# Projections of queries and keys in four column tiles of 32 instead of one product on the whole array, in both attentions of a two-layer macaron block

## The chip, the cores and the metric

The kernel runs on one core of a Trainium2 chip. The metric is the device time of one execution in microseconds: the median of 3 runs. A profile of one further execution shows what each engine did. TensorE is the matrix engine (PE in the profile; its weight loads are PEld), VectorE is DVE, ScalarE is ACT, GpSimd is POOL, SyncE is SP. All arithmetic is in f32.

## The reference

The input x is 2 x 2048 x 256. Six layers are added to it one after the other, each on a layer norm of x:

```python
x = x + 0.5 * L0_ffn(layernorm(x))    # mixture of 6 experts (top 2) plus a shared one
x = x + L0_attn(layernorm(x))         # full attention, 16 heads of 16
x = x + 0.5 * L0_ffn(layernorm(x))
x = x + 0.5 * L1_ffn(layernorm(x))    # gated recurrence of 2 steps, then tanh
x = x + L1_attn(layernorm(x))         # causal, rotary, relative positions within 32
x = x + 0.5 * L1_ffn(layernorm(x))
```

The change concerns the first products of the two attentions, for each of the 2 sequences:

```python
q = x @ Wq.T * (1.0 / sqrt(256))      # L0; in L1 the scale is 1/4, behind the rotation
k = x @ Wk.T
scores = einsum('bqhd,bkhd->bhqk', q, k)
attn = softmax(scores)
out = einsum('bhqk,bkhd->bqhd', attn, v)
```

In the second attention q and k are rotated in pairs of neighbouring features before the scores.

## The kernel before

x stays in on-chip memory for the whole run, in 32 chunks of 128 tokens; a block is 4 chunks (512 tokens). The normed input of a block is turned so that features lie on partitions: `xnT`, two tiles of 128 features x 512 tokens.

**One projection.** Heads are handled in groups of 4 (`G` = 4 groups). The weights are laid out so that one product of 128 output columns holds two groups: on each strip of 32 partitions lie the 16 features of one head of one group and the 16 of a head of the other. `mm2` (L143 to L149) makes such a product: two matmuls, one for each 128 input features, into one PSUM bank of 128 x 512, on the whole 128 x 128 array. The profile's records have two MATMULs and two LDWEIGHTS for each f32 matmul, so a call of `mm2` is 4 of each. ScalarE then makes two tiles from the bank, one for each group, with a scale of 0 for the other group's rows (`part_rows`, L137). In the second attention `rotate` (L1009) copies the bank first, VectorE shuffles neighbouring rows, and the rotation is done by VectorE or GpSimd; `keys_out` and `queries_out` split the groups later.

**What surrounds it.** Every instruction goes out in the order of the program text; each engine works through its own list. The work of an attention is cut into half steps. In one half step of the first attention (loop at the end of `attention0`), TensorE gets, in this order:

- for each of 4 heads, a score product for the exponentials (`exponential`, L770: keys as weights, 512 queries stream) and one for the row maxima (`largest`, L756: queries as weights, 512 keys stream). These use 32 rows and 128 columns of the array, heads side by side on different rows;
- the jobs that are due in this step, from a list by step number (`jobs.at`): projections of later queries and keys, values (L604), transposes (L635, L658, L672, L125), output products (L681);
- the values weighted with the exponentials of an earlier half step (`weighted`, L782): 4 heads, each 128 rows and 32 columns of the array, side by side on different columns, into 32 partitions each of one bank.

In the second attention the order within a half step is: transposes of the band with the relative positions (L1218, L1222), score products (L1201, L1208, L1123), weighted values (L1237), and then the due jobs.

VectorE takes the maxima from PSUM (L760, L1131), ScalarE the exponentials (L775, L1229) and the copies of the weighted values (L644). All PSUM banks come from one pool of 8 (`bank()`), in order of use.

**The calls.** There are 64 calls in the two attentions: in each, 16 of queries (one for two groups of heads of a block) and 16 of keys. The callers are `keys` (L727) and `queries` (L746) of `attention0`, and `rotate` (L1013) of `attention1`. `mm2` itself stays for the shared expert and the recurrences. The router's product (`route`, L203) has a form of its own: for each half of the features, four products of 32 columns, into 32 partitions each of one bank; its four products stream four different tiles.

Of the kernel before, what the change touches and what calls it, by code (L numbers as in the profile page):

```python
# [17 lines left out]
P = 128  # L18
# [24 lines left out]
def macaron_kernel(ctx: ExitStack, tc: tile.TileContext, t: dict, out: bass.AP):  # L43
    nc = tc.nc
# [28 lines left out]
    def bank():  # L73
        return psum.tile([P, TB], F32, name="s")
# [59 lines left out]
    def rows(j):  # L134
        return slice(32 * j, 32 * j + 32)

    def part_rows(dst, src, i, bias):  # L137

        nc.scalar.activation(
            dst, src, AF.Identity, scale=rowsel[:, i : i + 1], bias=0.0 if bias is None else bias  # L140
        )

    def mm2(ps, w, cols, rhs, start=True, stop=True):  # L143

        for kc in range(2):
            nc.tensor.matmul(  # L146
                ps, lhsT=w[:, kc, cols], rhs=rhs[:, kc, :],
                start=start and kc == 0, stop=stop and kc == 1,
            )  # L149

# [14 lines left out]
    def moe(w, ws, gate_w, gate_b, rev, tri, iota, z, behind, last, gathered):  # L167
# [3 lines left out]
        with ExitStack() as s:  # L171
# [147 lines left out]
            def shared_part(b, i):  # L319
                ps = bank()  # L320
                mm2(ps, ws[:, :, i // 2 * D : i // 2 * D + D], ts(i % 2, P), xnT[b])
                if i < 2:
                    sgs = wk.tile([P, TB], F32, name="sgs", bufs=6)
                    nc.scalar.activation(sgs, ps, AF.Silu)
                    ps = sgs
                half.setdefault(b, []).append(ps)
# [380 lines left out]
    def attention0(norm, tail, rest, wq, wk_, wv, wo, bff):  # L707
# [7 lines left out]
        with ExitStack() as s:  # L715
            z = Pieces(s, "a0", norm, wo, bff)
# [7 lines left out]
            def keys(b, g, qc):  # L724

                pk = bank()
                mm2(pk, wk_, ts(g // 2, P), z.xnT(b, qc))  # L727
                for i in range(2):
                    if qc == 0:
                        kT[b, g + i] = kpool.tile([P, S], F32, name="kT", bufs=5)  # L730
                    part_rows(kT[b, g + i][:, ts(qc, TB)], pk, i, rowsel[:, 2 + i : 3 + i])
# [10 lines left out]
            def queries(t):  # L742

                b, qc, g = groups[t]
                pq = bank()
                mm2(pq, wq, ts(g // 2, P), z.xnT(b, qc))  # L746
                for i in range(2):
                    q[t + i] = wk.tile([P, TB], F32, name="q", bufs=4)
                    part_rows(q[t + i], pq, 4 + i, None)
                    mx[t + i] = wk.tile([P, CPB * J, SB], F32, name="mx", bufs=4)  # L750
# [42 lines left out]
            for b in range(B):  # L793
                first = b * SB * G * PER

                for qc in range(SB) if b else ():
                    for c in range(CPB):
                        at(first - 43 + 4 * qc + c, z.ln_stats, b, qc, c)
                    at(first - 37 + 4 * qc, z.ln_transpose, b, qc)
                for qc in range(0 if b else SB):  # L800
                    norm.xn.pop(qc)
                    at(-1, z.add_bias, qc)
                for g in range(0, G, 2):
                    for qc in range(SB):
                        at(first - 7 + PER * g + qc if b else (qc if g else -1), keys, b, g, qc)
                for half in range(2):
                    for qc in range(SB):
                        due = first + 1 + 16 * half + qc if b else 4 * half + qc
                        at(due, vals, b, half, qc)
            for t, (b, qc, g) in enumerate(groups):  # L810
                if t % 2 == 0:
                    at(PER * t - 2, queries, t)
                at(PER * t + 18, z.divide, t, b, qc, g, True)
                if g == G - 1:
                    at(PER * t + 19, z.outputs_T, b, qc)
                    at(PER * t + 20, z.outputs, b, qc, 0)
                    at(PER * t + 20, z.outputs, b, qc, 1)
# [161 lines left out]
    def attention1(norm, tail, w, relk, relv, kbias, dramp, skew):  # L979
# [4 lines left out]
        with ExitStack() as s:  # L984
            z = Pieces(s, "a1", norm, w["o"], None)
# [23 lines left out]
            def rotate(xa, wa, b, qc, g):  # L1009


                pa = bank()
                mm2(pa, wa, ts(g // 2, P), z.xnT(b, qc))  # L1013
                nc.scalar.copy(xa, pa)
                xb = wk.tile([P, TB], F32, name="s2", bufs=4)
                nc.vector.stream_shuffle(xb, xa, [i ^ 1 for i in range(32)])

                if step < 0:
                    nc.vector.tensor_tensor(xa, xa, cos[b, qc], ALU.mult)
                    nc.vector.tensor_tensor(xb, xb, sin[b, qc], ALU.mult)  # L1020
                    nc.vector.tensor_tensor(xa, xa, xb, ALU.add)
                else:
                    op = nc.gpsimd.tensor_tensor
                    z.later(1, op, xa, xa, cos[b, qc], ALU.mult)
                    z.later(2, op, xb, xb, sin[b, qc], ALU.mult)
                    z.later(3, op, xa, xa, xb, ALU.add)
# [3 lines left out]
            def keys(b, qc, g, own):  # L1030

                if qc == 0:
                    pair = features_slot()
                    kT[b, qc, g], kT[b, qc, g + 1] = pair[:, 0, :], pair[:, 1, :]
                    packed[b, qc, g] = kT[b, qc, g + 1]
                elif own:
                    packed[b, qc, g] = wk.tile([P, TB], F32, name="s2", bufs=4)
                else:
                    packed[b, qc, g] = keys_tile(b, qc, g + 1)
                rotate(packed[b, qc, g], w["k"], b, qc, g)  # L1040
# [22 lines left out]
            def queries(t):  # L1063

                b, qc, g = groups[t]
                for i in range(2):
                    q[t + 1 - i] = wk.tile([P, TB], F32, name="q", bufs=6)
                    mx[t + i] = wk.tile([P, CPB, J, MX], F32, name="mx", bufs=2)
                rotate(q[t + 1], w["q"], b, qc, g)
# [201 lines left out]
            for n, (b, qc, g) in enumerate(groups):  # L1271
                size = 2 * (qc + 1)
                start = Me[-1] + 1 if n else 0
                free = Es[n - NBAND] + (4 if groups[n - NBAND][1] else 2) if n >= NBAND else -9
                start = max(start, free + 5 - size)
                if n > 5 and n % 2 == 0:
                    start = max(start, Ee[n - 5] + 5)
# [3 lines left out]
                start = Me[-1] + 2  # L1281
                if n:
                    start = max(start, Ee[-1] + 1)
# [318 lines left out]
```

## Time and profile before

| | us |
|---|---|
| median of 3 runs | 4071.13 |
| lowest, highest | 4068.05, 4072.09 |
| the profiled execution | 4068.88 |
| its span on the core | 4067.0 |
| first attention, about | 340 to 2000 |
| second attention, about | 2570 to 3760 |

The granted clock of TensorE was 0.993 of full speed over the span. The costliest groups of matmuls in the page (line, engine, operation, names, rows*columns of the array, shape, count | busy us, mean ns of one | idle time before):

```profile
L756 PE MATMUL s<-kT,q 32*128 32x512 f32 x4096 | 1018.6, 618 | 1.9 <-DVE mx L760 1.9
L770 PE MATMUL s<-q,kT 32*128 32x512 f32 x4096 | 1013.0, 615 | 0.4 <-DVE q L639 0.4
...
L782 PE MATMUL s<-pT,v 128*32 128x512 f32 x4096 | 549.8, 605 | 0.6 <-ACT pT L775 0.2
```

In the names, the streamed tile stands ahead of the weights. A matmul that streams 512 columns is in flight for about 600 ns, but the next one of the same form starts before it is over; busy time counts the union. Four that lie side by side on different rows or columns of the array run at the same time, so a busy time is less than count times mean.

Times "at" a place are microseconds from the start of the span.

### The profile page before, as it was taken

The page shows a single profiled execution, that of the slowest core. Times are in us where ns is not written, and L with a number is a line of the kernel's source. Part 1 is how long each engine was busy: PE and PEld are TensorE (multiplying, and loading weights), DVE is VectorE, ACT ScalarE, POOL GpSimd, SP SyncE. Part 2 cuts the span into 40 slices and gives each one's busy share as a digit, 9 for nine tenths or more (in the row PEclk, how much of TensorE's full clock was granted, in tenths as well). Part 3 has the DMA queues.
Part 4 walks back from the last instruction along what each step waited for, and adds up shares of the span by engine and source line. Part 5 has one row for each costly group of instructions (what it writes and reads, how often), then busy time and mean ns, then how long its engine had stood idle before and what let it go on. Part 6 is the DMA issues. An engine that isn't in the chain of part 4 may idle for free.

```text
span 4067.0 us, 76436 instructions
## 1 busy us (share of the span) xinstructions
PE 3996.5 (98%) x28256; PEld 1930.7 (47%) x28256; DVE 2701.9 (66%) x6128; ACT 2568.8 (63%) x5227; POOL 1634.8 (40%) x1456
## 2 busy tenths in 40 slices
PE   8999999999999999999999999999999999999999
PEld 4665333333344333333356655555554455554445
DVE  6247888888866888888752444667677766677533
ACT  2333788888887888888833322366667766667832
POOL 4245333336333333333442340345635645544410
PEclk9999999999999999999999999999999999999999
DMA  7341000100000000000033420334533344442101
GB/s 256 122 128 58 1 1 1 48 1 1 1 1 1 1 1 1 1 1 1 10 110 126 129 76 0 78 82 104 111 71 74 82 81 87 91 96 49 45 22 42
DMA packets 355508, 223.18 MB, mean 55 GB/s; under 512 B 146624, under 2 KB 338496, under 8 KB 355136
## 3 DMA queue, kind: packets, MB, share of 16 engines
q1 hardware_dynamic: 276800, 176.33, 16.5%
q0 software_dynamic: 12288, 33.57, 2.6%
q10 hardware_dynamic: 66048, 8.39, 1.3%
q8 instruction: 225, 3.69, 0.4%
q14 instruction: 147, 1.20, 0.1%
HBM read 113.12 MB, written 105.12 MB: 54 GB/s over the span
## 4 chain that ended last, share of the span: by engine, by line
PE 90%; DVE 5%; POOL 1%; ACT 1%; issue 1%; DMA 0%; SPq 0%; POOLq 0%; ACTq 0%; DVEq 0%
PE s L770 13%; PE s L782 12%; PE s L756 10%; PE s L146 10%; PE s L1237 7%; PE s L1123 6%; PE s L383 6%; PE s L1208 6%; PE s L403 3%; PE s L681 2%; PE s L1222 1%; PE s L1201 1%; PE s L1218 1%; PE s L344 1%; PE s L931 1%
## 5 line engine op out<-in xcount | busy, mean ns | idle before, releaser
L542 POOL TENSOR_TENSOR part<-part 128x512 f32<-128x512 f32 (+3 forms) x800 | 962.0, 1203 | 1389.9 <-ACT part L644 1377.0
L760 DVE TENSOR_REDUCE mx<-s 128x1 f32<-128x512 f32 x2048 | 1271.0, 684 | 292.8 <-PE s L756 292.6
L775 ACT ACTIVATE pT<-s 128x512 f32<-128x512 f32 x2048 | 1063.6, 618 | 200.7 <-PE s L756 199.1
L756 PE MATMUL s<-kT,q 32*128 32x512 f32 x4096 | 1018.6, 618 | 1.9 <-DVE mx L760 1.9
L770 PE MATMUL s<-q,kT 32*128 32x512 f32 x4096 | 1013.0, 615 | 0.4 <-DVE q L639 0.4
L1229 ACT ACTIVATE pT<-s 128x512 f32<-128x512 f32 (+3 forms) x1280 | 587.8, 542 | 252.8 <-PE s L1208 102.0
L770 PEld LDWEIGHTS s<-q,kT 32*128 32x128 f32 x4096 | 417.8, 183 | 466.9 <-DVE mx L760 327.0
L644 ACT COPY part<-s 128x512 f32<-128x512 f32 (+3 forms) x864 | 508.2, 589 | 148.2 <-PE s L782 60.2
L1131 DVE TENSOR_REDUCE mx<-s 128x1 f32<-128x512 f32 (+1 forms) x768 | 473.0, 679 | 132.3 <-PE s L1123 123.9
L782 PE MATMUL s<-pT,v 128*32 128x512 f32 x4096 | 549.8, 605 | 0.6 <-ACT pT L775 0.2
L756 PEld LDWEIGHTS s<-kT,q 32*128 32x128 f32 x4096 | 406.4, 184 | 128.9 <-ACT pT L775 76.2
L1123 PE MATMUL s<-kT,q 32*128 32x512 f32 (+7 forms) x2240 | 332.1, 433 | 0.0
L1237 PE MATMUL s<-pT,v 128*32 128x512 f32 (+3 forms) x2560 | 304.7, 541 | 9.1 <-DVE mx L1131 5.0
L383 PE MATMUL s<-we,xT 128*128 x592 | 278.7, 593 | 0.2 <-ACT xT L378 0.2
L390 DVE TENSOR_TENSOR h<-sg,s 128x256 f32<-128x256 f32 x148 | 62.4, 422 | 289.5 <-ACT sg L388 289.3
L1123 PE MATMUL s<-b,q 32*128 32x512 f32 (+7 forms) x1280 | 243.0, 518 | 1.6 <-DVE v L612 1.4
L782 PEld LDWEIGHTS s<-pT,v 128*32 128x32 f32 x4096 | 82.1, 108 | 336.1 <-ACT pT L775 300.4
L1147 DVE CUSTOM_DVE_ANT_0 band<-s,band 128x160 f32<-128x160 f32 (+1 forms) x512 | 155.7, 314 | 127.2 <-PE s L1208 62.6
L542 POOL TENSOR_TENSOR band<-band,mneg 128x640 f32<-128x640 f32 x128 | 161.3, 1260 | 189.2 <-DVE mneg L1157 127.9
L1208 PE MATMUL s<-q,kT 32*128 32x512 f32 (+3 forms) x1152 | 236.3, 509 | 0.0
L436 POOL DMA_INDIRECT yg<-results,at x128 | 123.8, 967 | 235.0 <-DMA results<-y 197.6
L1208 PE MATMUL s<-q,b 32*128 32x512 f32 (+3 forms) x896 | 208.5, 568 | 0.0
(227 smaller groups left out, 5148.1 us busy)
## 6 DMA issues: line engine op xcount, KB each, us to landing
band<-skew SPq DMA_DIRECT2D x32, 1280.0 KB, 7.5
pd<-band SPq DMA_DIRECT2D x32, 1280.0 KB, 8.5
xs<-places SPq DMA_DIRECT2D x148, 128.0 KB, 2.2
results<-y SPq DMA_DIRECT2D x148, 128.0 KB, 1.7
places<-zero SPq DMA_DIRECT2D x2, 4736.0 KB, 16.4
we<-in_we SPq DMA_DIRECT2D x12, 768.0 KB, 11.6
skew<-s ACTq DMA_DIRECT2D x32, 256.0 KB, 3.0
s<-pd SPq DMA_DIRECT2D x32, 256.0 KB, 4.3
```

Source lines behind the costliest of these rows:

```text
L383: nc.tensor.matmul(pu, lhsT=xT[n][:, ts(kc, P)], rhs=w[:, kc, ds(val[n], 2 * D)], start=kc == 0, stop=kc == 1,)
L542: fn(*args)
L644: nc.scalar.copy(part[:, q0:], pv[:, q0:])
L756: nc.tensor.matmul(ps, lhsT=q[t][rows(j), ts(qb, P)], rhs=kT[b, g][rows(j), ts(kc, TB)], start=True, stop=True,)
L760: nc.vector.tensor_reduce(mx[t][:, qb * J + j, kc : kc + 1], ps, AX.X, ALU.max)
L770: nc.tensor.matmul(st, lhsT=kT[b, g][rows(j), ts(kb, P)], rhs=q[t][rows(j), :], start=True, stop=True,)
L775: nc.scalar.activation(z.pTs[t, kb, j], st, AF.Exp)
L782: nc.tensor.matmul(pv[rows(j), :], lhsT=v[b, g // 2][:, kb, ds(h * VW, 32)], rhs=z.pTs.pop((t, kb, j)), start=True, stop=True,)
L1123: nc.tensor.matmul(ps[:, ds(cols, n)], lhsT=lhsT, rhs=kT[b, c, g][rows(j), ds(k0, n)], start=True, stop=True,)
L1208: nc.tensor.matmul(ps[:, q0:], lhsT=k, rhs=q[t][rows(j), q0:], start=True, stop=True, skip_group_check=True,)
L1229: nc.scalar.activation(z.pTs[t, kb, j][:, q0:], st.pop((t, kb, j))[:, q0:], AF.Exp)
L1237: nc.tensor.matmul(pv[rows(j), q0:], lhsT=v[b, kb // CPB, g // 2][:, kb % CPB, ds(h * VW, 32)], rhs=z.pTs.pop((t, kb, j))[:, q0:], start=T ...
```

## The change

A helper `mm2_cols` makes the same product as `mm2` in eight matmuls: for each half of the input features, four of 32 weight columns, each into its own 32 partitions of the bank. All four stream the same tile. The order is that of the router's product. The three callers use it; nothing else changes.

```diff
+    def mm2_cols(ps, w, col, rhs):
+
+        for kc in range(2):
+            for j in range(4):
+                nc.tensor.matmul(
+                    ps[rows(j), :], lhsT=w[:, kc, ds(col + 32 * j, 32)], rhs=rhs[:, kc, :],
+                    start=kc == 0, stop=kc == 1,
+                )
...
             def keys(b, g, qc):
 
                 pk = bank()
-                mm2(pk, wk_, ts(g // 2, P), z.xnT(b, qc))
+                mm2_cols(pk, wk_, g // 2 * P, z.xnT(b, qc))
...
                 pq = bank()
-                mm2(pq, wq, ts(g // 2, P), z.xnT(b, qc))
+                mm2_cols(pq, wq, g // 2 * P, z.xnT(b, qc))
...
                 pa = bank()
-                mm2(pa, wa, ts(g // 2, P), z.xnT(b, qc))
+                mm2_cols(pa, wa, g // 2 * P, z.xnT(b, qc))
                 nc.scalar.copy(xa, pa)
```

## The prediction

> **What bounds the kernel now.** I read the busy shares of the page first, then its chain of waits.
>
> ```profile
> PE 3996.5 (98%) x28256; PEld 1930.7 (47%) x28256; DVE 2701.9 (66%) x6128; ACT 2568.8 (63%) x5227; POOL 1634.8 (40%) x1456
> ...
> PE 90%; DVE 5%; POOL 1%; ACT 1%; issue 1%; DMA 0%; SPq 0%; POOLq 0%; ACTq 0%; DVEq 0%
> ```
>
> TensorE is busy 98% of the span and carries 90% of the chain. Ends of matmuls are modelled, so "busy" doesn't prove it; the test is whether its steps repeat to the nanosecond. In the first attention, 377 half steps that hold only 4 score products of each kind and 4 weighted values run 2924 to 2935 ns from the 0th to the 75th percentile: nothing but TensorE's own order sets them. So I look at single matmuls, in the timeline of TensorE around one query projection (start, length, engine, line, operation, rows*columns of the array):
>
> ```profile
> 742.66 0.59 PE L756 MATMUL s<-kT,q 32*128 32x512 f32 x1
> 743.18 1.98 PE L146 MATMUL s<-b,a_q 128*128 128x512 f32 x4
> 745.10 1.07 PE L782 MATMUL s<-pT,v 128*32 128x512 f32 x8
> 746.09 0.69 PE L770 MATMUL s<-q,kT 32*128 32x512 f32 x1
> ```
>
> Three forms follow each other: scores in row tiles (32*128), the projection on the whole array (128*128), weighted values in column tiles (128*32). One f32 matmul is two MATMUL records, so a projection is 4. Over the whole trace the start-to-start times of 512-column matmuls are: 429 ns inside one form (995 pairs of 128*128), but 522 ns from the last matmul of one form to the first of another (517 after row tiles). **A change of form costs 93 ns.** A second cost follows it: the first weight load no longer hides under a matmul. After a change the second 128*128 matmul starts 533 ns after the first instead of 429 (+104); in the 128*32 form it is 453 (+24), because 32 columns load in 106 ns and 128 in 190.
>
> The form that the change uses is in the trace: the router's product (L203) has the same two-by-four loop, 16 records of 128x512 f32. In the groups of TensorE by form (count | busy us, mean ns | idle before):
>
> ```profile
> L146 PE MATMUL s<-b,a_q 128*128 128x512 f32 x128 | 64.5, 627 | 0.4 <-ACT kT L1014 0.2
> ...
> L203 PE MATMUL s<-b,gate_w 128*32 128x512 f32 x64 | 7.7, 598 | 0.0
> ```
>
> Four L203 calls in 7.7 us are 1.92 us each; 32 query projections in 64.5 us are 2.02 us. The records of one L203 call start in four waves of four, at 0, 453, 882 and 1311 ns, members of a wave 7 ns apart. So column tiles run four abreast, and 16 narrow records take four pitches, as four wide ones do. Its weight loads, in the timeline of that queue, show why they don't count:
>
> ```profile
> 28.94 0.16 PEld L203 LDWEIGHTS s<-b,gate_w 128*32 128x32 f32 x8 [0.76 <-issue]
> 29.40 0.13 PEld L203 LDWEIGHTS s<-b,gate_w 128*32 128x32 f32 x4 [0.30 <-issue]
> 29.83 0.13 PEld L203 LDWEIGHTS s<-b,gate_w 128*32 128x32 f32 x4 [0.30 <-issue]
> ```
>
> Twelve of 16 begin at or just behind a wave that is then streaming, for the wave after.
>
> **The change, call by call.** 64 projections change form (32 in each attention). The stream itself stays at four pitches of 429 ns. What changes is the form to the left and the right, so I took all 64 from the trace with their neighbours.
>
> - **A, scores | projection | weighted: 22 calls, all in the first attention.** Old: 1914 ns from the first matmul to that of L782 (533+430+429+522), on every one of them. New: 453 + 3 x 429 = 1740, as L782 goes on in the same form; and L782's first pitch falls from 453 to 429. Gain 174 + 24 = 198 ns. 22 x 0.198 = **4.4 us**.
> - **B, weighted | projection | scores: 17 calls, all in the second attention**, where the due jobs run behind the weighted values. Old: 522 + 1914. New: no change ahead, and each tile follows its own predecessor by 429 (a wave's first follows the last of the wave ahead by 409): gain 113. Then 3 x 429 + 20 (the wave's stagger) + 522 = 1829: gain 85. 17 x 0.198 = **3.4 us**.
> - **C, weighted | projection | whole array: 8 calls** (transposes or output products next). Gain 113 ahead; the block is 1829 for 1821; but the next operation now pays the entry: 165 for 109 ns at 128 columns (6 calls), 320 for 215 at 256 (2). Net gain 6 x 0.05 + 0 = 0.3 us.
> - **D, scores on both sides: 7 calls.** 453 + 2 x 429 + 20 + 522 = 1853 for 1914: gain 0.06 each. Only 5 of them lie where TensorE runs without a wait just after: 0.3 us.
> - **Lost: whole array on one or both sides.** A form that was one run is broken. The 5 calls at the first attention's start, as one run, lose 93 + 24 + 20 = 0.14; the 3 at the second's start 93 + 137 + 56 = 0.29; one at 2753 us 0.14; one between scores and output products (1264 us) 32 + 105 = 0.14. Sum 0.7 us.
>
> All through: 4.4 + 3.4 + 0.3 + 0.3 - 0.7 = 7.7 us.
>
> **What comes through.** A saved pitch counts only if TensorE isn't waiting next. After 22 of 22 calls of A there is no stall over 40 ns in the next 25 us. ScalarE and VectorE have room there: from 340 to 2000 us VectorE is busy 1353 and ScalarE 1335 of 1660 us, and in an A half step both still have 4.6 us for the work of a 2.9 us one plus two copies of the projection. I take all of it. In the second attention (VectorE 825, ScalarE 783 of 1190 us) stalls follow: behind the calls from 2649 us on I find 90 to 160 ns a few us later in most cases, 300 to 800 ns in some, mostly on a bank that VectorE's maximum (L1131) holds. Where VectorE's backlog began before the call, the gain is eaten there; where it began behind it, VectorE's work moves up too. The bounds for B are 0 and 3.4 us; as the releaser is under 70% busy, its backlogs are short, and I take 2.8. The two starts run into waits of 1.4 to 2.0 us right behind (359.9 and 2592.3 us), so their loss of 0.43 us, and D's gain of 0.06 among it, vanish. Sum: 4.4 + 2.8 + 0.3 + 0.2 - 0.3 = **7.4 us**.
>
> **Edits at nothing.** 768 more matmuls and 768 more loads (4 records of each become 16, 64 times) start 7 ns apart in the shade of a 429 ns wave; without that cover 12 x 7 x 64 = 5.4 us. No DMA, copy, wait or buffer is added; the bank's one wait stays ahead of the first load, and its readers (two scaled copies, or one copy) can start 592 ns after the fourth wave, at about 1.93 us instead of 1.98. The finish order in other queues is untouched.
>
> [...] One cost the trace does not show: L203 and L782 stream four different tiles into the four column tiles; here all four stream the same one. [...] The row has four tiles in one pitch of 429, so the measurement of this kernel decides: nothing lost, for different tiles. For the same tile the cost lies between nothing and full serialising (256 x 3 x 429 ns = 329 us); below nothing is out, since a wave still streams 512 columns. L203 is nearest by form, so I take nothing.
>
> **The sum against the time.** The profiled execution took 4068.9 us (span 4067.0), the median of the three runs is 4071.1, within 4068.1 to 4072.1. 7.4 us off the profiled one gives 4061.5; off the median, **4063.7 us**, 0.18% less. A measurement of this kernel can tell about 0.2% (8.1 us) from no change, so my forecast stands just inside "no change".
>
> **Rivals.**
> 1. *Half of it is eaten:* the second attention's stalls take all of B. For it: L1131 is 2.7% of the chain there, and L1237 waits 21 times for it. Against: VectorE is busy 69% of that stage, and its backlog moves up where it begins behind a call. 4071.1 - 4.6 = 4066.5. Chance 0.2.
> 2. *More than counted:* all of B comes through, and waits of under 40 ns behind changed forms go too: 8 to 11 us, 4061. For it: the sum without any loss by waits is already 7.7. Against: the three runs' spread is 4 us, as large as the excess. Chance 0.2.
> 3. *The four streams of one tile hinder each other.* Place: each of the 256 waves. [...] It decides from 7.4 us / 256 = 29 ns a wave on (7% of a pitch); from 61 ns on the kernel is slower by over 0.2%. Against: the router's row. Chance 0.1.
> 4. *It doesn't do what it says:* the waves of one call don't overlap with the weighted values (a drain between two runs of one form, say at the wait on the bank). Then A and B gain 80 to 105 ns: 39 x 0.09 = 3.5, less 0.4: 4068. Against: 429 ns inside the form in L203 and L782. Chance 0.05.
>
> The forecast itself has 0.45. **The range**: its own, with the spread of the runs, is 4060.5 to 4067; rivals 1, 2 and 4 lie at 4058 to 4070. I give 4058 to 4071, which leaves out rival 3 and some edges. Faster by over 0.2% (below 4063.0): a third of the forecast's weight (0.15) and most of rival 2 (0.17) make 0.32. Slower by over 0.2%: most of rival 3 and a little for what I don't see, 0.1. Within: 0.58.
>
> **What would show it.** In the profile after: L146 loses its 256 records of a_q and a_k, and a new line has 1024 of 128*32; each call takes 1.92 us alone; from its first matmul to L782's 1.74 us instead of 1.92 (A), and from L1237's last to the projection's first 0.41 instead of 0.52 (B); half steps with a query fall from 4.84 to 4.64 us; L604, L681 and L658 behind a projection pay an entry. It is wrong if waves come at over 429 ns, if L782 still starts its second wave at 453 ns behind a projection, or if the second attention keeps its length while the first loses 4 us.

## The result, and the profile after

The changed kernel takes 4062.93 us in the median of 22 runs (4061.28 to 4065.99), the kernel before 4068.67 us (4066.74 to 4072.09, 22 runs beside it). The ratio is 0.9986, with a 95% interval from 0.998 to 0.9993: 5.7 us less, within the 0.2% that I had called no change. A second session, on a chip where the kernel before takes 4194.7 us, gave 0.9997 (0.9988 to 1.0005). Both intervals hold the 4.1 us that the sum over stages below comes to; the second also holds no change at all.

The page after, busy shares and chain of waits:

```profile
PE 3989.4 (98%) x29024; PEld 1922.0 (47%) x29024; DVE 2699.4 (66%) x6128; ACT 2569.8 (63%) x5227; POOL 1634.7 (40%) x1456
...
PE 90%; DVE 5%; POOL 1%; issue 1%; ACT 1%; DMA 1%; SPq 0%; POOLq 0%; DVEq 0%; ACTq 0%
```

768 more matmul records, and TensorE is busy 7 us less. The other engines do the same work as before. TensorE by form (L155 is the new helper's line; lines below it have moved by 9):

```profile
L155 PE MATMUL s<-b,a_k 128*32 128x512 f32 x512 | 62.1, 609 | 0.0
L155 PE MATMUL s<-b,a_q 128*32 128x512 f32 x512 | 61.3, 596 | 0.4 <-ACT kT L1023 0.2
```

61.3 us for 32 calls are 1.92 us each, as foretold. The same query projection as in the prediction, in TensorE's timeline:

```profile
743.99 0.59 PE L765 MATMUL s<-kT,q 32*128 32x512 f32 x1
744.51 1.92 PE L155 MATMUL s<-b,a_q 128*32 128x512 f32 x16
746.25 0.61 PE L791 MATMUL s<-pT,v 128*32 128x512 f32 x4
```

The weighted values (L791) start 1.74 us after the projection, not 1.92: case A within 2 ns (1740 to 1742 by the records on 22 of 22 calls, foretold 1740). So each local claim held. But setting each matmul of the changed kernel beside the same one of the kernel before, in the two profiled executions, shows where the gain went. The table says how much later the changed kernel is at each place (negative: it is earlier). A half-clock window is a stretch in which the trace shows a granted clock of 0.50:

| place in the kernel before, us | later (+) or earlier (-), us | what lies between |
|---|---|---|
| 340 | +0.58 | ahead of any change |
| 440 | +1.40 | start of the first attention; half-clock windows placed differently (before at 364 and 409 us, 3.4 us each; after at 410 us, 6.8 us) |
| 1900 | +0.93 | 15 queries and 7 keys of case A; one projection ahead of output products, 0.14 lost |
| 2640 | +0.89 | experts, recurrence, start of the second attention |
| 2740 | +0.47 | three calls of B and C |
| 2760 | -1.03 | a half-clock window that only the kernel before has here (2753.7 us, 3.4 us long) |
| 3680 | -4.10 | the other calls of B and C |
| 4060 | -5.29 | a half-clock window at 3870 in the kernel before (3.4 us long) |

22 calls of A, worth 4.4 us by my sum, brought 0.6 us (0.5 with the projection at 1264 us, whose loss of 0.14 us was foretold). The calls of B and C brought 3.5 us of 3.7.

### The profile page after: what moved, and what is told of

It reads as the page before. It is cut to its first block, busy times and chain, and to the rows that moved or that the text cites. A ratio compares the mean times of both kernels' runs of the same rounds, so it can differ in the third digit from the quotient of the medians.

```text
span 4061.7 us, 78003 instructions
## 1 busy us (share of the span) xinstructions
PE 3989.4 (98%) x29024; PEld 1922.0 (47%) x29024; DVE 2699.4 (66%) x6128; ACT 2569.8 (63%) x5227; POOL 1634.7 (40%) x1456
## 4 chain that ended last, share of the span: by engine, by line
PE 90%; DVE 5%; POOL 1%; issue 1%; ACT 1%; DMA 1%; SPq 0%; POOLq 0%; DVEq 0%; ACTq 0%
PE s L779 13%; PE s L791 12%; PE s L765 10%; PE s L146 7%; PE s L1246 7%; PE s L1132 6%; PE s L392 6%; PE s L1217 6%; PE s L412 3%; PE s L155 2%; PE s L690 2%; PE s L1231 1%; PE s L1210 1%; PE s L353 1%; PE s L1227 1%
## 5 line engine op out<-in xcount | busy, mean ns | idle before, releaser
L653 ACT COPY part<-s 128x512 f32<-128x512 f32 (+3 forms) x864 | 508.1, 589 | 150.4 <-PE s L791 61.3
L791 PE MATMUL s<-pT,v 128*32 128x512 f32 x4096 | 549.3, 604 | 0.6 <-ACT pT L784 0.2
L791 PEld LDWEIGHTS s<-pT,v 128*32 128x32 f32 x4096 | 84.3, 108 | 332.7 <-ACT pT L784 300.5
```

The costliest lines, as they stand in the source:

```text
L653: nc.scalar.copy(part[:, q0:], pv[:, q0:])
L791: nc.tensor.matmul(pv[rows(j), :], lhsT=v[b, g // 2][:, kb, ds(h * VW, 32)], rhs=z.pTs.pop((t, kb, j)), start=True, stop=True,)
```

## Where A's gain goes

The half steps of the first attention tell it. The length from one weighted product to the next, median over calls with no other job:

| half step | before | after |
|---|---|---|
| with a query | 4849 ns | 4675 ns |
| the next one, after a query | 2951 | 3095 |
| the next one, after a key | 3133 | 3277 |
| none near | 2927 | 2927 |

The half step with the projection gives 174 ns, and the next takes 144 back, where it should have given the other 24 (I had put these with the query's own half step, at 4.64 us). What it waits for stands in the timeline of weight loads, and stood there in the kernel before:

```profile
746.63 0.20 PEld L770 LDWEIGHTS s<-q,kT 32*128 32x128 f32 x2
746.99 0.25 PEld L756 LDWEIGHTS s<-kT,q 32*128 32x128 f32 x2 [0.16 <-ACT part L644]
```

One of the four row-maximum products (L756) waits for ScalarE's copy of the weighted values (L644). The banks are used in turn, 8 of them: behind the bank of the weighted values come those of three row maxima and four exponentials, and the fourth row maximum is the eighth, so it needs that bank again. Now ScalarE's timeline (L139 makes the two copies of the projection), kernel before:

```profile
745.20 1.26 ACT L139 ACTIVATE q<-s,rowsel 128x512 f32<-128x512 f32 x2 [0.67 <-PE s L146]
746.36 0.59 ACT L644 COPY part<-s 128x512 f32<-128x512 f32 x1
```

and the changed kernel:

```profile
746.50 1.26 ACT L139 ACTIVATE q<-s,rowsel 128x512 f32<-128x512 f32 x2 [0.64 <-PE s L155]
747.66 0.58 ACT L653 COPY part<-s 128x512 f32<-128x512 f32 x1
```

ScalarE idles 0.6 us for the projection's end, makes two copies, and then the copy that frees the bank. From the projection's first matmul (743.18 and 744.51) the first copy starts after 2.02 and 1.99 us: its last matmul ends only 60 ns sooner (1.92 for 1.98 us), since the gain is at the borders (453 + 3 x 429 = 1740 ns to the weighted values, for 533 + 430 + 429 + 522), not in the stream, where both forms have a pitch of 429 ns. The bank is free at +3.77 and +3.73 us. TensorE wants it 0.2 us sooner than before, and stands:

```profile
748.19 0.60 PE L779 MATMUL s<-q,kT 32*128 32x512 f32 x2
748.29 0.91 PE L765 MATMUL s<-kT,q 32*128 32x512 f32 x2
748.62 0.60 PE L779 MATMUL s<-q,kT 32*128 32x512 f32 x2
748.83 0.59 PE L765 MATMUL s<-kT,q 32*128 32x512 f32 x1
```

The wave starts at 748.19, its fourth member at 748.29 with its load in the open, and that one's second half comes at 748.83, 0.2 us behind the rest of its wave. The next weighted product waits for all. So the theory is a chain: the projection's end, two copies, the copy of the weighted values, the bank. Its engine, ScalarE, has idle time (it is busy 1335 of 1660 us from 340 to 2000 us), but ahead of the chain. The experiments test it.

## The experiments

Each timed experiment has its own ratio, to the kernel before on the same chip. The first four, and the last two, ran on chips where the kernel before takes 4194 us. The half steps above have the same lengths there, within 2 ns; in the profiles of the changed kernel, the longer time is spent ahead of the first attention (some 70 us) and between the two (some 55). Why is open.

**1. The first attention alone.** `rotate` keeps `mm2`:

```diff
-                mm2_cols(pa, wa, g // 2 * P, z.xnT(b, qc))
+                mm2(pa, wa, ts(g // 2, P), z.xnT(b, qc))
```

> Only the first attention's 32 projections are in column tiles; the second attention keeps the whole-array product. My prediction's sum for this stage was 4.4 us gained (22 calls of A at 0.198, and small change). Theory now: A's gain is taken back in the next half step, because the fourth row-maximum product needs the PSUM bank of the weighted values, whose copy on ScalarE stands behind the two copies of the projection, and these start at the projection's end, which comes only 0.06 us earlier. Then 22 x 0.03 = 0.7 us are left, about 4068.0 if before is at 4068.7, and A blocks in the trace show 1741 ns, but half steps with a query stay at 4.84 us. Rival (the gain is real there and the loss lies in the second attention): 4064.3.

Measured: 4194.99 us for 4194.43, ratio 1.0002 (0.9993 to 1.001). Half steps with a query 4676 ns, the next 3095. A gain of 4.4 us would be 0.99895, outside the interval. The loss is in this stage, as the theory has it; only the foretold "half steps with a query stay at 4.84" was loosely put: it is the pair of half steps that stays.

**2. The second attention alone.** The two callers of `attention0` keep `mm2`:

```diff
-                mm2_cols(pk, wk_, g // 2 * P, z.xnT(b, qc))
+                mm2(pk, wk_, ts(g // 2, P), z.xnT(b, qc))
...
-                mm2_cols(pq, wq, g // 2 * P, z.xnT(b, qc))
+                mm2(pq, wq, ts(g // 2, P), z.xnT(b, qc))
```

> Only the second attention's 32 projections are in column tiles. Theory: here the full gain comes through, 17 x 0.198 + 0.3 = 3.7 us, about 4065.0 if before is at 4068.7; from the first call in the steady part (2649 us) to the last (3672 us) the trace is 3.5 us shorter apart from places where the clock is halved. Rival (stalls on VectorE's maxima eat part of it, as the prediction had it): 2.8 + 0.3 us or less, 4065.6 or more; if the first attention has its full gain, less than 1.3 us here.

Measured: 4191.88 us for 4194.43, ratio 0.9992 (0.9984 to 1.0). The trace is sharper than the time: from the first of the last 25 projections to the last it is 997.78 us here and 1000.93 in experiment 1, neither with a half-clock window in it. By the prediction's terms this stretch holds the gain of 16 calls of B (3.2 us), five of C (0.2) and the lost one at 2753 us (-0.1), 3.3 in all. 3.15 us came: next to nothing is eaten. The chain of the first attention is not there, as the weighted values stand ahead of the projection, and ScalarE copies them first. In the changed kernel, at the call of 3036.68 us:

```profile
3036.99 0.58 ACT L653 COPY part<-s 128x512 f32<-128x512 f32 x1 [0.28 <-PE s L1246]
3038.65 0.58 ACT L1023 COPY kT<-s 128x512 f32<-128x512 f32 x1 [1.08 <-PE s L155]
```

The bank of the weighted values is free 1 us before the projection ends. No experiment moved these copies; this is read from the trace.

**3. Shorten the chain: one projection copy on VectorE.** `part_rows` gets a flag; the calls of A set it for the second copy.

```diff
+        if vector:
+            nc.vector.tensor_scalar(
+                dst, src, rowsel[:, i : i + 1], 0.0 if bias is None else bias, ALU.mult, ALU.add
+            )
+            return
...
-                    part_rows(q[t + i], pq, 4 + i, None)
+                    part_rows(q[t + i], pq, 4 + i, None, i == 1 and t > 0)
```

> The changed kernel, with the second of the two copies of a projection moved from ScalarE to VectorE, in the first attention for all calls of A (queries from the second on, keys of the second sequence). Theory: the chain ahead of the copy of the weighted values is 0.6 us shorter, the bank is free before the fourth row-maximum product wants it, and 22 x 0.17 = 3.7 us come through beyond the changed kernel: 4059.2 if that is at 4062.9; half steps with a query at 4.64 us. Rival (TensorE itself loses the time behind the column tiles): no gain, 4063. Rival (VectorE is the next bound): slower than the changed kernel, as 22 x 0.69 us are added to an engine that is busy 1352 of 1660 us.

Measured: 4185.32 us for 4194.43, ratio 0.9981 (0.9974 to 0.9987). The half step after a query takes 2901 ns (3095 in the changed kernel), after a key 2979 (3277). The time that TensorE lost was the chain's: with it shortened, the full 24 ns of the cheaper entry come through behind queries (2901 for 2925). Behind keys 78 ns are still missing; experiment 9 shows where.

**4. The same move without column tiles**, the control:

> The kernel before, with the same copies moved to VectorE: the control for the run with both. Theory: the bank of the weighted values was free some 70 ns ahead of its need here, so nothing is gained: within 1 us of before. Rival (the move is worth 3 to 4 us by itself, whatever the form of the projection): 4065.

Measured: 4191.41 us for 4194.43, ratio 0.9991 (0.9982 to 0.9999). My expectation missed: half steps after a query went from 2951 to 2925 ns, after a key from 3133 to 2925. The bank had no 70 ns to spare in the kernel before; it was late already, by 26 ns behind queries and 208 behind keys. Times 15 and 7 that is 1.8 us, inside the interval of the time (0.4 to 7.5 us). The keys' copies explain the difference between the two: with a bias they take 773 ns for 684 (means in ScalarE's groups of the kernel before), twice 89 ns more. I had read the margin off one load that came 70 ns ahead of its matmul, without seeing that this lane's second load was then in the open.

**5. Lengthen the chain**, in the kernel before:

```diff
                     part_rows(q[t + i], pq, 4 + i, None)
+                    if i == 1 and t > 0:
+                        part_rows(q[t + i], pq, 4 + i, None)
```

> The kernel before, whole-array projections, with one more copy on ScalarE behind the two of a query projection (it writes the same tile again), 15 times in the first attention. The half step behind a query projection takes 2951 ns there, 26 more than one without, so the chain (projection's end, copies, copy of the weighted values, bank) ends last already. Theory: each further copy of 0.58 us makes that half step 0.58 us longer, to 3.5 us, and the whole 15 x 0.58 = 8.7 us slower. Rival (ScalarE has 20% of its time free there and takes it up): no more than 1 us.

Measured: 4076.59 us for 4069.21, ratio 1.0021 (1.0013 to 1.0029). The half step after a query is 3673 ns, 722 longer. In ScalarE's timeline one such place:

```profile
648.61 1.99 ACT L139 ACTIVATE q<-s,rowsel 128x512 f32<-128x512 f32 x3 [0.68 <-PE s L146]
650.50 0.58 ACT L644 COPY part<-s 128x512 f32<-128x512 f32 x1
```

Three copies take 1.99 us where two take 1.26, so the third adds 0.73 us, not 0.58, and all of it reaches TensorE: 15 x 0.72 is 10.8 us, and the interval of the time is 5.3 to 11.8. The rival, that ScalarE's free time takes it up, is out.

**6. Which bank?** In the changed kernel, the copy of the weighted values behind a projection goes to VectorE; the projection's copies stay.

```diff
-            nc.scalar.copy(part[:, q0:], pv[:, q0:])
+            if self.busy:
+                nc.vector.tensor_copy(part[:, q0:], pv[:, q0:])
+            else:
+                nc.scalar.copy(part[:, q0:], pv[:, q0:])
+            self.busy = False
```

(`busy` is set by the calls of A.)

> The changed kernel, both copies of the projection on ScalarE as they are, but the copy of the weighted values that stands behind them moved to VectorE in those 22 half steps (and one more). If the wait is for the bank of the weighted values, as the theory has it, this frees it as well as the moved projection copy did: half steps behind a query at 2900 ns instead of 3095, 3 us in all for queries, and up to 0.37 us for each of 7 keys: 4 to 5.5 us under the changed kernel, a ratio near 0.9975 to before. If the wait is for the bank of the projection itself, it stays at 3095 and nothing is gained.

Measured: 4060.07 us for 4069.21, ratio 0.9975 (0.9965 to 0.9986). Half steps after a query 2974 ns, after a key 2975. The load of the late row maximum now follows VectorE's copy (L655):

```profile
650.31 0.20 PEld L772 LDWEIGHTS s<-kT,q 32*128 32x128 f32 x2 [0.17 <-DVE part L655]
```

So it is the bank of the weighted values. I had expected 2900: VectorE's copy starts as soon as the weighted values are there and takes 690 ns, where ScalarE's takes 585, and by the records the late lane's load begins 27 ns ahead of its matmul. Its second load is then exposed; the half step is 73 ns longer than in experiment 3.

**7. The kernel before once more**, one profile:

> The kernel before, profiled again. Both theories: half steps behind a query 2951 ns, behind a key 3133; the distance between the 25 last projections of the second attention 1000.9 us plus 1.4 to 1.7 us for each window of halved clock that falls into it.

2953 and 3134 ns, and 1000.97 us with no half-clock window in the stretch. The first profile of the kernel before has one there (2753.7 us) and 1002.56.

**8 and 9. The changed kernel and the one of experiment 3, side by side.**

> The changed kernel once more, beside the next one on the same chip. Theory: by half steps, 15 queries x 0.028 + 7 keys x 0.029 + 3.2 us of the second attention's last 25 projections and 0.3 us ahead of them, about 4.1 us under before, a ratio of 0.999, if windows of halved clock fall alike in both.

> The changed kernel with the second copy of a projection on VectorE in the first attention, beside the changed one on the same chip. Theory: 15 x 0.194 + 7 x 0.298 = 5.0 us under the changed kernel (half steps behind a query 2901 for 3095 ns, behind a key 2979 for 3277), a ratio to before near 0.9978. Rival (VectorE's added 22 copies cost elsewhere what they free here): no more than 3 us under the changed kernel.

Measured: the changed kernel 4192.82 us, ratio 0.9997 (0.9988 to 1.0005); with VectorE's copy 4186.98, ratio 0.9982 (0.9975 to 0.9989), beside 4194.68 for the kernel before. 5.8 us apart, for 5.0 foretold by half steps. TensorE's timeline at one query of the latter (L160 projection, L799 weighted values, L773 the row maxima, L787 the scores for the exponentials):

```profile
717.22 1.92 PE L160 MATMUL s<-b,a_q 128*32 128x512 f32 x16
718.96 1.04 PE L799 MATMUL s<-pT,v 128*32 128x512 f32 x8
...
721.33 0.59 PE L773 MATMUL s<-kT,q 32*128 32x512 f32 x1
721.33 0.59 PE L787 MATMUL s<-q,kT 32*128 32x512 f32 x1
721.34 0.59 PE L773 MATMUL s<-kT,q 32*128 32x512 f32 x1
721.35 0.59 PE L787 MATMUL s<-q,kT 32*128 32x512 f32 x1
721.86 1.06 PE L799 MATMUL s<-pT,v 128*32 128x512 f32 x8
```

The last wave is whole again, all four within 0.02 us, and the next weighted product starts 2.90 us after the first. Behind a key it is not whole (L140 is VectorE's copy of the projection):

```profile
1198.30 0.81 DVE L140 TENSOR_SCALAR kT<-s,rowsel 128x512 f32<-128x512 f32 x1 [1.05 <-ACT kT L144]
1199.17 0.19 PEld L773 LDWEIGHTS s<-kT,q 32*128 32x128 f32 x2
```

VectorE's copy of the keys starts when ScalarE's first one is over, and the late load begins 53 ns behind its end, at each of the seven keys; ScalarE's copy of the weighted values was over 0.12 us before that end. So VectorE's copy ends last there, and 78 ns of each such half step (2979 for 2901) stay lost. The row maximum may be held by the exponential just ahead of it in TensorE's order, which gets the projection's bank; that is not shown. By the medians this version is faster than both kernels.

## Why the prediction was right, and where not

- **Time and sign.** 4063.7 us foretold, 4062.93 measured, inside the range; "within 0.2%" had the largest chance and is what came. The gain foretold from the median shown then was 7.4 us, the measured one 5.7 (2.8 to 8.1), by the half steps and stages 4.1 (0.6 in A, 3.5 in B and C). That the time came within 1 us of the forecast is luck: the gain was too large in the sum, and the median of three runs, from which it was taken off, was 2.5 us above that of 22. Between 5.7 and 4.1 us the times can't tell.
- **The price of a change of form** (93 ns, and 104 or 24 ns for the entry): right on every call. A's block is 1741 ns in the median, B's 1830 and 409 ahead of it, D's 1854, against 1740, 1829, 409 and 1853.
- **One tile streamed into four column tiles:** nothing lost; the waves come at 0, 453, 883 and 1312 ns. Rival 3 is out: no run shows a cost of four streams of one tile, and a wave follows the one ahead by 429 ns, as one whole-array matmul follows another.
- **What comes through, first attention: wrong.** "After 22 of 22 calls of A there is no stall over 40 ns ... I take all of it." The stall was there at each call, 26 ns behind queries, under my bound, and 208 behind keys, which the bound hid because I allowed for an exposed load at every wave. And the argument from room ("both still have 4.6 us for the work") was of the wrong kind: ScalarE has idle time, but it comes ahead of the projection's end (0.64 us at the call shown), where it can't be used. The term A of 4.4 us measured 0.6.
- **What comes through, second attention: mis-sized.** I took 2.8 of B's 3.4 us; nearly all came. The waits on VectorE's maxima that I saw behind the calls moved up with them: the weighted values wait 21 times for them before, 4.8 us in all, and 21 times, 4.8 us, after. And the weighted values are copied before the projection's end, so their bank does not hang on it.
- **Edits at nothing** named the mechanism and passed it by: "its readers can start ... at about 1.93 us instead of 1.98". Read as a wait and not as a cost, that line is the reason why a call of A can't gain more than some 50 ns; it gained 29 ns.

## What to carry to other kernels

When a step on the bound engine gets shorter, look up which of its results end sooner, not only when the engine goes on: a consumer that starts at the step's end and frees a buffer for the next step can take the gain back, even with idle time of its own. Here it took back 144 of 174 ns, with ScalarE busy 1335 of 1660 us. Half steps that are all alike but for the one behind the step (2951 for 2927 ns) were the sign of such a chain, and 24 ns of it were enough. Put products of the same form next to each other (a border cost 93 ns here), and give the chain behind them two engines (worth 5.8 us here).

## What the hardware showed that I had not expected

**Half-clock windows move between executions.** At one place of the second attention the kernel before, in windows of its trace (PE busy, loads, DVE, ACT, POOL, granted clock, DMA share, GB/s):

```profile
2755.00:2758.00 3.00, 3.00 (x11) 0.73 (x10) 1.86 (x5) 0.89 (x3) 0.08 (x1) 0.65 0.97 247
```

and its timeline there:

```profile
2753.10 0.33 PE L635 MATMUL s<-ident,mneg 128*128 128x128 f32 x1 [1.31 <-DVE mneg L1157]
2753.27 3.19 PE L146 MATMUL s<-b,a_q 128*128 128x512 f32 x4
```

Behind a wait of 1.31 us the granted clock is 0.50 from 2753.69 us on, for 3.41 us, and the projection takes 3.19 us for 1.98; the changed kernel waits 1.31 us at the same place and keeps a granted clock of 1.00 (2750 to 2760 us). In the traces of two executions of the kernel before, the windows at 0.50 are 3.41 us long, or 2 or 3 times that (6.83 and 10.24 us), apart from the one that the end cuts off; there are 12 and 10, 59 and 49 us in all. One in the dense stretch of the last 25 projections costs 1.4 to 1.7 us (1002.56 for 1000.95 us; 999.15 and 999.49 for 997.78). Whether the wait of 1.31 us brings the window on is not shown. A change of 4 us in a kernel of 4070 is seen in the lengths of its half steps long before it is seen in its time.

**A change of form had the same price at every place looked at, in f32:** between 512-column matmuls 93 ns at the border (522 for 429; 88 behind row tiles) and the first weight load in the open (24 ns for 32 columns; at 128 columns 104 ns ahead of 512-column matmuls and 56 ahead of 128-column ones). Between two lines of one form it was nothing: the projection and L791 follow each other at the pitch of 429.
